# A graph-attention kernel: adding weight tiles by half transfers, finishing a sum one block later, and moving small transfers to another queue

## The chip, the cores and the metric

The kernel runs on one core of one Trainium2 chip. The metric is the device time of one execution in microseconds (us), from the first to the last instruction; lower is better. TensorE (PE) does the matrix products, VectorE (DVE) and ScalarE (ACT) the elementwise work, GpSimd (POOL) issues the transfers that add or cast, SyncE (SP) the plain loads. Each engine works through its own instructions in order and waits on semaphores for the others.

## The reference

Two layers over 4096 nodes with 512 features and 4 heads of 128. The first layer is an encoder and a decoder that share one masked attention; the second is a graph attention network (GAT). Cut to what matters here, the GAT is

```python
feats  = einsum('nf,hfo->hno', X, W)                 # 4 heads of 128
logits = leaky_relu(e_s[:, :, None] + e_n[:, None, :], 0.2)
attn   = softmax(logits + NEG_INF * (1 - A), axis=-1) # 4096 x 4096 for each head
out    = relu(einsum('hnm,hmo->hno', attn, feats) + b)
```

and the encoder's attention, `softmax(sigmoid(f1 + f2))` over the masked neighbours, has the same shape: unnormalised weights for every pair of nodes, a weighted sum of values, and the sum of the weights as the denominator. All of it is float32.

## The kernel before, in words

One function, `attention` (L211), is used three times: as "enc" (the encoder, `kept="write"`), "dec" (the decoder, `kept="read"`, without denominators) and "gat" (the last one, `kept=None`). It walks over 8 blocks, 4 heads times 2 halves of 2048 target nodes. A block has 32 steps `j`, one for each group of 128 source nodes. A step makes one weight tile `e` of 128 sources by 2048 targets (1 MB): in gat ACT does a Relu (L820) and DVE multiplies by the mask tile `a` (L821); in enc ACT does Tanh and Exp (L422, L423) and DVE multiplies (L424). Then PE multiplies the values of the 128 sources with the four 512-wide parts of `e` into four PSUM banks (L352; the fourth bank is taken up at step `EVICT` = 2, and its parts of steps 0 and 1 are done then, L349).

The denominators are the sums of `e` over all sources. A tile can be summed in three ways, and a pair of tuples for each block, `(moved, by_ones)`, says which steps go which way:

- steps in `moved`: a transfer issued by POOL adds the tile onto a second sum tile, `sums2` (L364, with `accum_op` add; the first one only copies). In gat `sums2` is the 1 MB of `w`, named `row0`; in its first block, where `w` still holds the row of scores, it is a tile in device memory, `dacc`, read back into a weight tile at step 30 (L322).
- steps in `by_ones`: PE multiplies the tile by a matrix of ones into the denominators' bank `den` (L304, `add_to_den`).
- all others: DVE adds the tile onto `acc` (L370, L372). In gat `acc` is half of `R[2]`, so these lines read `R<-R,e`.

At the end of the block PE adds `sums2` and `acc` into `den` too. In gat the tuple is `((0, 2, 5, 7, 10, 12, 15, 17, 20, 22, 25), (9, 30, 31))` for every block: 11 tiles by transfer, 3 by ones, 18 by DVE.

Weight tiles rotate through 9 slots (7 and 2 of another pool). A slot is free when PE, DVE and, for a moved tile, the transfer have read it. Mask tiles have 5 slots.

What follows a block is spread over the next block's steps by `at(j, ...)`: eviction of the four banks at step 2 (`out_gat`, ACT, L826), the copy of `den` at `INVERT` = 4 (ACT, L248), and then a chain of small transfers through device memory that turns the sums into a column (`dcol`), inverts it on DVE (L255, L256), stores it (`rinvs`) and spreads it over the partitions (`rb`, four tiles of 256 KB, L262). DVE multiplies by `rb` (L830), ACT adds the bias (L833) and POOL adds the result onto the output in device memory (L839). All these hops are issued by POOL, in the same queue as the moved tiles. The order of instructions within an engine is set when the program is built, from priorities and from `issue_after` pins; it does not change at run time.

Of the kernel before, what the change touches and what calls it, by code (L numbers as in the profile page):

```python
# [31 lines left out]
FP = mybir.dt.float32  # L32
U8 = mybir.dt.uint8
AF = mybir.ActivationFunctionType
ALU = mybir.AluOpType
# [5 lines left out]
IB = 512  # L41
# [4 lines left out]
TB = 2048  # L46
# [15 lines left out]
ENC_FIRST = (), (6, 7, 14, 15, 22, 23, 30, 31)  # L62
ENC_SECOND = (13, 15, 17, 20, 22, 25), (5, 6, 10, 11, 30, 31)
ENC = (0, 2, 5, 7, 10, 12, 15, 17, 20, 22, 25), (8, 9, 30, 31)
GAT = (0, 2, 5, 7, 10, 12, 15, 17, 20, 22, 25), (9, 30, 31)

KEEP = 5

# [13 lines left out]
def kernel(ctx, tc, x, xT, adjT, w0, w0T, v0, wencT, wdecT, vecs, w1, w1T, a1, outT):  # L82
# [65 lines left out]
    ekeep = [[[dram.tile([P, TB], FP, name=f"ekeep{h}_{t}_{k}") for k in range(NJ // KEEP)] for t in range(NTB)]  # L148
             for h in range(H)]

    dacc = dram.tile([P, TB], FP, name="dacc")

    masks = [[dram.tile([MG * P, TB], U8, name=f"mask{t}_{g}") for g in range(NJ // MG)] for t in range(NTB)]

    def everywhere(d, row, lo, n):
# [55 lines left out]
    def attention(what, keep, pools, weights, values, row_of, out, finish, ebufs, modes=None, invert=None,  # L211
# [21 lines left out]
        spool, made, masks0 = pools, 0, list(masks0)  # L233
        if invert is not None:
            acc = spool.tile([P, TB], FP, name="acc") if sums is None else sums
            sums2 = spool.tile([P, TB], FP, name="acc2") if sums2 is None else sums2

        def weight_tile():
            nonlocal made
# [2 lines left out]
                return keep.tile([P, TB], FP, name="e", tag="ek", bufs=EP)  # L242
            return spool.tile([P, TB], FP, name="e", bufs=ebufs)

        def denominators(h, tb, den):

            dsb = spool.tile([P, IB], FP, name="dsb")
            (nc.vector.tensor_copy if kept is not None else nc.scalar.copy)(dsb, den)  # L248
            nc.gpsimd.dma_start(dens[h][tb], dsb[0:P:32, :])
            dcol = spool.tile([P, TB // P], FP, name="dcol", bufs=2)  # L250
            nc.gpsimd.dma_start(dcol, dens[h][tb].rearrange("s (q k) -> (s q) k", k=TB // P))
            return dcol

        def invert_them(h, tb, dcol):
            nc.vector.tensor_scalar(dcol, dcol, invert[0], None, invert[1])  # L255
            nc.vector.reciprocal(dcol, dcol)  # L256
            nc.gpsimd.dma_start(rinvs[h][tb].rearrange("o (p k) -> (o p) k", k=TB // P), dcol)

        def spread(h, tb, s):

            rb = spool.tile([P, IB], FP, name="rb", bufs=2)
            nc.gpsimd.dma_start(rb, everywhere(rinvs[h][tb], 0, s * IB, IB))  # L262
            return rb

        def at(j, f, *args):
# [3 lines left out]
        def ending(h, tb, po, den, slack):  # L269

            outs = [out(spool, h, tb, s, po[s]) for s in range(SB)]
            if den is not None:
                def invert_later():
                    dcol = denominators(h, tb, den)
                    at(INVERT + slack + 6, invert_them, h, tb, dcol)

                at(INVERT, invert_later)
            rbs = {}
            for s, o in enumerate(outs):

                j = INVERT + slack + 7 + s % 2 + s // 2 * 7
                at(j, lambda s=s: rbs.update({s: spread(h, tb, s)}))
                for k, f in enumerate(finish):
                    at(j + 6 + k, lambda f=f, s=s, o=o: f(spool, h, tb, s, o, rbs[s], False))

        def next_row_of(h, tb):
            rowb = keep.tile([P, TB], FP, name="rowb", bufs=2)
# [5 lines left out]
        blocks = [(h, tb) for h in range(H) for tb in range(NTB)]  # L293
        for n, (h, tb) in enumerate(blocks):
            last = n == len(blocks) - 1
            moved, by_ones = modes(n) if modes is not None else ((), ())
            if invert is not None:
                den = bank1()
                begun = False

            def add_to_den(t, stop=False):
                nonlocal begun, last_ones
                for s in range(SB):
                    last_ones = nc.tensor.matmul(den[s * 32:(s + 1) * 32, :], ones[:, 0:32], t[:, s * IB:(s + 1) * IB],  # L304
                                                 start=not begun, stop=stop)
                begun = True

            po, ahead = [bank() for _ in range(SB - 1)], []
            adds, held, back, stores, next_row = [], [], None, [], None
            for j in range(NJ):  # L310

                with pinned(products_of):
                    for f in later.pop(j, []):
                        f()
                with pinned([a_load, *products_of] if j else []):
                    if (n, j) in extras:
                        extras[n, j](a_load)
                    if not last and j == NJ - 10:
                        next_row = next_row_of(*blocks[n + 1])
                if n == 0 and moved and j == NJ - 2:  # L320
                    back = weight_tile()
                    nc.gpsimd.dma_start(back, dacc)  # L322
                e = weight_tile()
                store = j % KEEP == KEEP - 1 and kept is not None
                if store and kept == "read":
                    a_load = nc.sync.dma_start(e, ekeep[h][tb][j // KEEP])
                else:
                    if masks0:
                        a, a_load = masks0.pop(0)
                    else:  # L330
                        a = mask_tile(keep)
                        a_load = load_mask(a, tb, j)
                    products_of = weights(e, rowb, a, j, h, SB if n + j == 0 else 1)
                    if store:
                        stores.append((j // KEEP, e))

                    if j % KEEP == KEEP - 3 and stores:
                        k, t = stores.pop()
                        nc.scalar.dma_start(ekeep[h][tb][k], t)

                def products():
                    nonlocal last_main, last_ones

                    with tc.issue_after(last_ones.ins) if last_ones is not None else nullcontext():

                        if j == EVICT:
                            po.append(bank())
                            for k, t in ahead:
                                nc.tensor.matmul(po[-1], block(values[h], k), t[:, (SB - 1) * IB:SB * IB],  # L349
                                                 start=(k == 0), stop=False)  # L350
                        for s, b in enumerate(po):
                            last_main = nc.tensor.matmul(b, block(values[h], j), e[:, s * IB:(s + 1) * IB],  # L352
                                                         start=(j == 0), stop=(j == NJ - 1))
                    last_ones = None


                early = last and j == NJ - 1 and invert is not None
                if not early:
                    products()
                if j < EVICT:  # L360
                    ahead.append((j, e))
                if invert is not None:
                    if j in moved:
                        nc.gpsimd.dma_start(sums2 if n else dacc, e, **({"accum_op": ALU.add} if j > moved[0] else {}))  # L364
                    elif j in by_ones:
                        held.append(e)
                    else:
                        adds.append(e)
                        if len(adds) == 2:
                            nc.vector.tensor_add(acc, *adds)  # L370
                        elif len(adds) > 2:
                            nc.vector.tensor_add(acc, acc, e)  # L372

                    if held and j + 1 not in by_ones:
                        with tc.issue_after(last_main.ins):
                            for t in held:
                                add_to_den(t)
                        held = []
                    if j == NJ - 1:
                        with tc.issue_after(last_ones.ins) if last_ones is not None else nullcontext():  # L380
                            if moved:
                                add_to_den(sums2 if n else back)
                            add_to_den(acc, True)
                if early:
                    products()
            for k, t in stores:
# [4 lines left out]
            if not last:  # L391

                at(EVICT, ending, h, tb, po, den if invert is not None else None,
                   4 if kept == "write" and n == 0 else 0)
                rowb = next_row
                continue
            outs = [out(spool, h, tb, s, po[s]) for s in range(SB)]
# [4 lines left out]
                        f(spool, h, tb, s, o, rb, True)  # L402
                continue

            inv = spool.tile([P, IB], FP, name="dsb")
            nc.vector.tensor_scalar(inv, den, invert[0], None, invert[1])
            nc.vector.reciprocal(inv, inv)
            if kept is not None:
# [432 lines left out]
    with tc.tile_pool(name="gat", bufs=1) as spool:  # L841
        x1_last = []

        def load_last(load):
# [1 line left out]
            nc.sync.dma_start(x1_last[0], outT[(H - 1) * P:H * P, (NTB - 1) * TB:NTB * TB])  # L846

        attention("gat", spool, spool, gat_weights, v1, lambda h, tb: (rowsg, tb * H + h), out_gat,
                  (scaled_gat, add_to_output), 7, lambda n: GAT, (N * TINY, ALU.add), sums=R[2][:, 0:TB],
                  sums2=row0, row0=row0,  # L850
                  extras={(0, 1): rest_of_rows, (H * NTB - 1, NJ - 10): load_last})


# [40 lines left out]
```

## Time and profile before

| | before |
|---|---|
| time, median of 3 runs | 3289.51 us (3280.21 to 3290.55) |
| profiled run | 3281.28 us, span 3279.5 us, granted clock 0.995 |
| PE busy | 3200.3 us (98%) |
| DVE busy | 2691.2 us (82%) |
| ACT busy | 2598.6 us (79%) |
| gat, block after block | from 2350 us to the end |
| enc, block after block | from 70 us to 1048 us |

Busy time is averaged over stages with different limits, so the table only says that several engines are nearly full. The stages have to be read one by one: the windows of the blocks, the chain of waits, and for each engine what ended its idle time. PE is counted in records, and one 512-wide product in float32 leaves two of them.

### The profile page before, as it was taken

How to read it: one execution, taken by the hardware profiler on the slowest of the kernel's cores; microseconds unless marked ns; L12 is line 12 of the kernel's file. 1: busy time of each engine (PE TensorE's matmuls, PEld its weight loads, DVE VectorE, ACT ScalarE, POOL GpSimd, SP SyncE). 2: the span in 40 equal slices, each digit the busy share in tenths (PEclk: the TensorE clock that was granted, in tenths of full speed). 3: DMA queues.
4: the chain of work that ended last, by engine and by line, in shares of the span. 5: the costliest groups of instructions: out<-in, count | busy, mean ns of one | idle time of the engine just before them, and what ended most of it. 6: DMA issues, size and time to landing. Idle time of an engine off the chain costs nothing.

```text
span 3279.5 us, 25758 instructions
## 1 busy us (share of the span) xinstructions
PE 3200.3 (98%) x8775; PEld 1484.6 (45%) x8775; DVE 2691.2 (82%) x1923; ACT 2598.6 (79%) x1901; POOL 336.7 (10%) x484
## 2 busy tenths in 40 slices
PE   7999999999999999999999999999999999999999
PEld 6334434444443464444444444448644444444443
DVE  6999999999999665655665666586699999999997
ACT  7999999999997449999999999565756666666564
POOL 2000110110110000000000000024201111111111
PEclk9999999999999999999999999999999999999999
DMA  9998988988986013434443444242389789778876
GB/s 208 196 192 226 263 225 231 261 221 231 261 231 171 0 65 126 152 130 136 140 151 131 136 141 138 62 134 72 89 197 225 180 202 226 192 187 207 211 188 155
DMA packets 181028, 564.83 MB, mean 172 GB/s; under 512 B 20452, under 2 KB 23780, under 8 KB 144288
## 3 DMA queue, kind: packets, MB, share of 16 engines
q0 software_dynamic: 43952, 216.38, 34.3%
q1 hardware_dynamic: 126432, 293.72, 26.6%
q10 hardware_dynamic: 10512, 53.08, 4.0%
q8 instruction: 69, 1.13, 0.1%
q14 instruction: 63, 0.52, 0.0%
HBM read 378.15 MB, written 95.82 MB: 145 GB/s over the span
## 4 chain that ended last, share of the span: by engine, by line
PE 64%; DVE 13%; ACT 11%; issue 8%; DMA 4%; POOL 0%; ACTq 0%; DVEq 0%; SPq 0%; POOLq 0%
PE ps L352 50%; PE ps L579 7%; DVE e L424 7%; ACT e L422 6%; ACT e L423 4%; PE ps L763 3%; DVE acc L372 2%; DMA a<-mask 2%; DMA acc<-e 2%; PE den L304 1%; DVE R L372 1%; DVE e L821 1%; PE ps L635 1%; PE ps L349 1%; PE ps L503 1%
## 5 line engine op out<-in xcount | busy, mean ns | idle before, releaser
L352 PE MATMUL ps<-e,R 128*128 128x512 f32 x6048 | 2626.0, 595 | 44.4 <-DVE e L424 36.3
L352 PEld LDWEIGHTS ps<-e,R 128*128 128x128 f32 x6048 | 1145.1, 190 | 1516.7 <-issue 1416.4
L424 DVE TENSOR_TENSOR e<-e,a 128x2048 f32<-128x2048 f32 (+1 forms) x470 | 1052.2, 2260 | 382.0 <-ACT e L423 367.4
L422 ACT ACTIVATE e<-rowb,score 128x2048 f32<-128x2048 f32 (+1 forms) x470 | 912.7, 1968 | 101.8 <-PE ps L352 58.1
L423 ACT ACTIVATE e<-e 128x2048 f32<-128x2048 f32 (+1 forms) x470 | 871.0, 1879 | 6.5
L820 ACT ACTIVATE e<-rowb,nq,jcol 128x2048 f32<-128x2048 f32 x224 | 457.6, 2087 | 231.7 <-DMA w<-e 158.0
L821 DVE SCALAR_TENSOR_TENSOR e<-e,jcol,a 128x2048 f32<-128x2048 f32 (+1 forms) x259 | 591.3, 2317 | 2.6 <-ACT e L820 2.6
L372 DVE TENSOR_TENSOR acc<-acc,e 128x2048 f32<-128x2048 f32 x130 | 297.1, 2286 | 2.1
L372 DVE TENSOR_TENSOR R<-R,e 128x2048 f32<-128x2048 f32 x128 | 292.2, 2283 | 0.0
L579 PE MATMUL ps<-R,w 128*128 128x512 f32 x512 | 220.3, 592 | 0.6 <-DVE w L537 0.6
L262 POOL DMA_DIRECT2D rb<-rinvs x88 | 60.9, 723 | 1076.2 <-DVE R L527 870.5
L579 PEld LDWEIGHTS ps<-R,w 128*128 128x128 f32 x512 | 97.2, 190 | 122.7 <-issue 118.1
L364 POOL DMA_DIRECT2D w<-e x77 | 65.0, 844 | 639.2 <-DMA w<-e 210.4
L364 POOL DMA_DIRECT2D acc<-e x72 | 60.8, 844 | 593.8 <-DMA acc<-e 195.5
L763 PE MATMUL ps<-w1x,hT 128*128 128x260 f32 x512 | 118.5, 391 | 1.8 <-ACT hT L736 1.8
L599 ACT ACTIVATE ex<-ps,bias 128x512 f32<-128x512 f32 x64 | 44.0, 688 | 95.3 <-PE ps L579 78.2
L763 PEld LDWEIGHTS ps<-w1x,hT 128*128 128x128 f32 x512 | 98.6, 194 | 21.6 <-ACT hT L736 3.4
L820 ACT ACTIVATE e<-w,nq,jcol 128x2048 f32<-128x2048 f32 (+1 forms) x35 | 65.3, 1937 | 32.4 <-DMA dacc<-e 32.4
L601 DVE SCALAR_TENSOR_TENSOR ex<-ex,re 128x512 f32<-128x512 f32 x64 | 44.9, 701 | 35.6 <-ACT re L600 35.4
L833 ACT ACTIVATE R<-R,vec 128x512 f32<-128x512 f32 x32 | 23.0, 718 | 60.8 <-DVE R L830 60.6
L768 ACT ACTIVATE R<-ps,rstd 128x128 f32<-128x128 f32 x128 | 38.4, 370 | 38.0 <-PE ps L763 36.9
L304 PE MATMUL den<-e,ones 128*32 128x512 f32 x504 | 61.3, 599 | 0.0
(163 smaller groups left out, 1264.3 us busy)
## 6 DMA issues: line engine op xcount, KB each, us to landing
a<-mask SPq DMA_DIRECT2D x720, 256.0 KB, 3.7
w<-e POOLq DMA_DIRECT2D x77, 1024.0 KB, 8.2
acc<-e POOLq DMA_DIRECT2D x72, 1024.0 KB, 8.8
ekeep<-e ACTq DMA_DIRECT2D x48, 1024.0 KB, 6.2
e<-ekeep SPq DMA_DIRECT2D x48, 1024.0 KB, 4.8
rb<-rinvs POOLq DMA_DIRECT2D x88, 256.0 KB, 5.4
mask<-in_adjT POOLq DMA_DIRECT2D x8, 2048.0 KB, 100.7
rowb<-rows SPq DMA_DIRECT2D x16, 1024.0 KB, 6.5
```

Of the source, the lines that this page charges most:

```text
L262: nc.gpsimd.dma_start(rb, everywhere(rinvs[h][tb], 0, s * IB, IB))
L304: last_ones = nc.tensor.matmul(den[s * 32:(s + 1) * 32, :], ones[:, 0:32], t[:, s * IB:(s + 1) * IB], start=not begun, stop=stop)
L352: last_main = nc.tensor.matmul(b, block(values[h], j), e[:, s * IB:(s + 1) * IB], start=(j == 0), stop=(j == NJ - 1))
L364: nc.gpsimd.dma_start(sums2 if n else dacc, e, **({"accum_op": ALU.add} if j > moved[0] else {}))
L372: nc.vector.tensor_add(acc, acc, e)
L422: nc.scalar.activation(e, rowb, AF.Tanh, bias=column(score[:, 1], j, h), scale=0.5)
L423: last_act = nc.scalar.activation(e, e, AF.Exp, scale=0.5)
L424: last_dve = nc.vector.tensor_mul(e, e, a)
L579: nc.tensor.matmul(z, w[:, fb, o * P:(o + 1) * P], nodes(src[fb], ib), start=(fb == 0), stop=(fb == C - 1))
L763: nc.tensor.matmul(b[:, 0:2 * DX], hT[:, fb, c * P:(c + 1) * P], w1x[:, fb, 2 * k:2 * k + 2, :].rearrange("p h x -> p (h x)"), start=(fb = ...
L820: last_act = nc.scalar.activation(e, rowb, AF.Relu, bias=column(nq, j, h), scale=column(jcol, j, h))
L821: last_dve = nc.vector.scalar_tensor_tensor(e, e, column(jcol2, j, h), a, ALU.add, ALU.mult)
```

## The change

The change has these parts:

1. The transfers that add a moved tile are issued in two halves of 1024 columns each (`in_parts(2, into, e)`). This is in `attention` itself and so holds for enc as well as for gat.
2. In gat the tuples differ by block. The first block moves 13 tiles (even steps 0 to 24) and has two by ones. The middle six blocks move 13 tiles, odd steps 3 to 27, have two by ones, and carry a third entry, `True`. The last block moves 11 tiles, odd steps 3 to 23, and has three by ones as before, 12 in the place of 9.
3. Where the third entry is set, the moved sum is not added to `den` at the end of the block but in step 1 of the next one (`ends_later`).
4. In gat's first block the moved sum is the second half of `R[2]`, on the chip, in the place of `dacc` in device memory; the read back is gone.
5. In gat the hops of the denominators are issued by ACT in the place of POOL (`hop`), and set further apart: store at step 4, column at 7, inversion at 11, store of the inverses at 14, spreading at 15, 16, 20 and 21, scaling three steps after each, output six steps after each. In enc and dec they stay on POOL at the steps they had.
6. `dsb` and `rb` share one tag with 3 slots, where `dsb` had one and `rb` two.

It is for letting each half's transfer run while the other half's completion is awaited, so that more tiles can be summed by transfers, for giving the last of them time to land, and for keeping the small hops out of the queue of the moved tiles.

```diff
-GAT = (0, 2, 5, 7, 10, 12, 15, 17, 20, 22, 25), (9, 30, 31)
+GAT_FIRST = (0, 2, 4, 6, 8, 10, 12, 14, 16, 18, 20, 22, 24), (30, 31)
+GAT = tuple(range(3, 28, 2)), (30, 31), True
+GAT_LAST = (3, 5, 7, 9, 11, 13, 15, 17, 19, 21, 23), (12, 30, 31)
...
-    dacc = dram.tile([P, TB], FP, name="dacc")
...
+        hop = nc.scalar if kept is None else nc.gpsimd
...
-            dsb = spool.tile([P, IB], FP, name="dsb")
+            dsb = spool.tile([P, IB], FP, name="dsb", tag="rb", bufs=3)
             (nc.vector.tensor_copy if kept is not None else nc.scalar.copy)(dsb, den)
-            nc.gpsimd.dma_start(dens[h][tb], dsb[0:P:32, :])
+            hop.dma_start(dens[h][tb], dsb[0:P:32, :])
...
-            rb = spool.tile([P, IB], FP, name="rb", bufs=2)
-            nc.gpsimd.dma_start(rb, everywhere(rinvs[h][tb], 0, s * IB, IB))
+            rb = spool.tile([P, IB], FP, name="rb", bufs=3)
+            hop.dma_start(rb, everywhere(rinvs[h][tb], 0, s * IB, IB))
...
+                at(INVERT, denominators, h, tb, den)
+                at(INVERT + (0 if hop is nc.gpsimd else 3), columns, h, tb, dcols)
+                at(INVERT + slack + (6 if hop is nc.gpsimd else 7), invert_them, dcols)
+                at(INVERT + slack + (6 if hop is nc.gpsimd else 10), inverses, h, tb, dcols)
...
-                j = INVERT + slack + 7 + s % 2 + s // 2 * 7
+                j = INVERT + slack + (7 if hop is nc.gpsimd else 11) + s % 2 + s // 2 * (7 if hop is nc.gpsimd else 5)
...
-                    at(j + 6 + k, lambda f=f, s=s, o=o: f(spool, h, tb, s, o, rbs[s], False))
+                    at(j + (6 + k if hop is nc.gpsimd else 3 + 3 * k),
+                       lambda f=f, s=s, o=o: f(spool, h, tb, s, o, rbs[s], False))
...
-                if n == 0 and moved and j == NJ - 2:
-                    back = weight_tile()
-                    nc.gpsimd.dma_start(back, dacc)
...
-                        nc.gpsimd.dma_start(sums2 if n else dacc, e, **({"accum_op": ALU.add} if j > moved[0] else {}))
+                        for into_half, e_half in in_parts(2, into, e):
+                            nc.gpsimd.dma_start(into_half, e_half, **({"accum_op": ALU.add} if j > moved[0] else {}))
...
-                            if moved:
-                                add_to_den(sums2 if n else back)
-                            add_to_den(acc, True)
+                            if moved and not ends_later:
+                                add_to_den(den, into, not begun)
+                                begun = True
+                            add_to_den(den, acc, not begun, not ends_later)
...
+                if ends_later:
+                    at(1, add_to_den, den, into, False, True)
```

More of the change, by code (lines that the diff above doesn't have):

```diff
@@ L235, in attention @@
             acc = spool.tile([P, TB], FP, name="acc") if sums is None else sums
-            sums2 = spool.tile([P, TB], FP, name="acc2") if sums2 is None else sums2
+            sums2 = (spool.tile([P, TB], FP, name="acc2"), None) if sums2 is None else sums2
         def weight_tile():
@@ L243, in weight_tile, with add_to_den, columns, invert_them @@
             return spool.tile([P, TB], FP, name="e", bufs=ebufs)
+        hop = nc.scalar if kept is None else nc.gpsimd
+        def add_to_den(den, t, start=False, stop=False):
+            nonlocal last_ones
+            for s in range(SB):
+                last_ones = nc.tensor.matmul(den[s * 32:(s + 1) * 32, :], ones[:, 0:32], t[:, s * IB:(s + 1) * IB],
+                                             start=start, stop=stop)
         def denominators(h, tb, den):
-            dsb = spool.tile([P, IB], FP, name="dsb")
+            dsb = spool.tile([P, IB], FP, name="dsb", tag="rb", bufs=3)
             (nc.vector.tensor_copy if kept is not None else nc.scalar.copy)(dsb, den)
-            nc.gpsimd.dma_start(dens[h][tb], dsb[0:P:32, :])
+            hop.dma_start(dens[h][tb], dsb[0:P:32, :])
+        def columns(h, tb, dcols):
             dcol = spool.tile([P, TB // P], FP, name="dcol", bufs=2)
[L251 to L257, printed above, removed]
+            hop.dma_start(dcol, dens[h][tb].rearrange("s (q k) -> (s q) k", k=TB // P))
+            dcols.append(dcol)
+        def invert_them(dcols):
+            nc.vector.tensor_scalar(dcols[0], dcols[0], invert[0], None, invert[1])
+            nc.vector.reciprocal(dcols[0], dcols[0])
+        def inverses(h, tb, dcols):
+            hop.dma_start(rinvs[h][tb].rearrange("o (p k) -> (o p) k", k=TB // P), dcols[0])
         def spread(h, tb, s):
-            rb = spool.tile([P, IB], FP, name="rb", bufs=2)
-            nc.gpsimd.dma_start(rb, everywhere(rinvs[h][tb], 0, s * IB, IB))
+            rb = spool.tile([P, IB], FP, name="rb", bufs=3)
+            hop.dma_start(rb, everywhere(rinvs[h][tb], 0, s * IB, IB))
             return rb
@@ L272, in ending @@
             if den is not None:
[L273 to L277, printed above, removed]
+                dcols = []
+                at(INVERT, denominators, h, tb, den)
+                at(INVERT + (0 if hop is nc.gpsimd else 3), columns, h, tb, dcols)
+                at(INVERT + slack + (6 if hop is nc.gpsimd else 7), invert_them, dcols)
+                at(INVERT + slack + (6 if hop is nc.gpsimd else 10), inverses, h, tb, dcols)
             rbs = {}
             for s, o in enumerate(outs):
-                j = INVERT + slack + 7 + s % 2 + s // 2 * 7
+                j = INVERT + slack + (7 if hop is nc.gpsimd else 11) + s % 2 + s // 2 * (7 if hop is nc.gpsimd else 5)
                 at(j, lambda s=s: rbs.update({s: spread(h, tb, s)}))
                 for k, f in enumerate(finish):
-                    at(j + 6 + k, lambda f=f, s=s, o=o: f(spool, h, tb, s, o, rbs[s], False))
+                    at(j + (6 + k if hop is nc.gpsimd else 3 + 3 * k),
+                       lambda f=f, s=s, o=o: f(spool, h, tb, s, o, rbs[s], False))
         def next_row_of(h, tb):
@@ L295, in attention @@
             last = n == len(blocks) - 1
[L296 to L306, printed above, removed]
+            moved, by_ones, *ends_later = modes(n) if modes is not None else ((), ())
+            den = bank1() if invert is not None else None
+            begun = False
+            into = sums2[0 if n else 1] if moved else None
             po, ahead = [bank() for _ in range(SB - 1)], []
-            adds, held, back, stores, next_row = [], [], None, [], None
+            adds, held, stores, next_row = [], [], [], None
             for j in range(NJ):
@@ L376, in attention @@
                             for t in held:
-                                add_to_den(t)
+                                add_to_den(den, t, not begun)
+                                begun = True
                         held = []
@@ L380, in attention @@
                         with tc.issue_after(last_ones.ins) if last_ones is not None else nullcontext():
-                            if moved:
-                                add_to_den(sums2 if n else back)
-                            add_to_den(acc, True)
+                            if moved and not ends_later:
+                                add_to_den(den, into, not begun)
+                                begun = True
+                            add_to_den(den, acc, not begun, not ends_later)
                 if early:
@@ L403, in attention @@
                 continue
-            inv = spool.tile([P, IB], FP, name="dsb")
+            inv = spool.tile([P, IB], FP, name="dsb", tag="rb", bufs=3)
             nc.vector.tensor_scalar(inv, den, invert[0], None, invert[1])
@@ L848 @@
         attention("gat", spool, spool, gat_weights, v1, lambda h, tb: (rowsg, tb * H + h), out_gat,
-                  (scaled_gat, add_to_output), 7, lambda n: GAT, (N * TINY, ALU.add), sums=R[2][:, 0:TB],
-                  sums2=row0, row0=row0,
+                  (scaled_gat, add_to_output), 7, lambda n: (GAT_FIRST, *[GAT] * (H * NTB - 2), GAT_LAST)[n],
+                  (N * TINY, ALU.add), sums=R[2][:, 0:TB], sums2=(row0, R[2][:, TB:N]), row0=row0,
                   extras={(0, 1): rest_of_rows, (H * NTB - 1, NJ - 10): load_last})
```

## The prediction

> **What bounds the kernel now.** The change touches gat (all parts) and enc (the halves), so I read those two stages: first the windows of the blocks, then the chain of waits, then who waited for whom, then timelines of POOL and ACT. Gat's middle blocks and one of enc, with columns PE, PEld, DVE, ACT, POOL, clock, DMA share, GB/s:
>
> ```profile
> 2579.00:2694.00 115.00, 115.00 (x304) 49.56 (x296) 110.58 (x55) 71.36 (x43) 16.81 (x23) 1.00 0.83 199
> 2809.00:2924.00 115.00, 115.00 (x300) 49.57 (x296) 115.00 (x57) 71.10 (x42) 16.97 (x23) 1.00 0.85 205
> ...
> 450.00:570.00 120.00, 116.67 (x308) 49.42 (x304) 114.62 (x64) 119.87 (x65) 13.21 (x18) 1.00 0.86 237
> ```
>
> In gat PE has no gap and DVE hardly one; ACT has 44 us to spare. In enc ACT is full. Which of gat's two full engines sets the pace, the chain (start, length, what) says:
>
> ```profile
> 2455.14 2.36 DVE e L821
> 2457.50 0.04 issue
> 2457.54 3.70 PE ps L352 x8
> ...
> 2576.07 3.57 PE den L304 x32
> 2579.64 5.35 PE ps L352 x12
> 2584.99 1.72 PE ps L349 x4
> 2586.71 27.47 PE ps L352 x64
> 2614.17 1.00 PE den L304 x8
> 2615.17 75.73 PE ps L352 x176
> 2690.90 3.57 PE den L304 x32
> ```
>
> DVE carries the chain through the first block only, up to 2457.5; from there PE does, every block 2690.90 - 2576.07 = 114.83 us. All of that is matmuls: 110.3 us of products and five sums by ones, one alone (1.00 us, step 9) and four together (3.57 us, 0.89 each: steps 30 and 31, `w`, `acc`). So gat gets faster by what is taken off PE, and by nothing else.
>
> How near are the others? From the starts and ends of each `e`'s instructions in the trace: DVE finishes `e` 0.1 us before PE starts on it at the end of block 0 (there step 31 takes 4.43 us on PE in place of 3.43), 0.5 us at the end of block 2, 5.4 us at the end of block 6. ACT is 8 to 19 us ahead of DVE in blocks 2 and 3, 2.7 us at least in block 6; ACT's lead over PE as a whole stays near 22 us, which is the ring of 9 tiles. What holds ACT and POOL:
>
> ```profile
> POOL w L364 <- DMA w<-e: 210.4, 30, 8.4
> ACT e L820 <- DMA w<-e: 158.0, 46, 6.6
> POOL w L364 <- PE den L304: 134.0, 5, 29.0
> ACT R L833 <- DVE R L830: 60.6, 23, 8.3
> DVE R L830 <- DMA rb<-rinvs: 10.3, 6, 4.4
> ```
>
> The transfers are a loop of their own: each add waits for the one before it to land. Two of them on POOL:
>
> ```profile
> 2601.68 0.86 POOL L364 DMA_DIRECT2D w<-e  x1 [7.29 <-DVE dcol L255]
> 2610.23 0.86 POOL L364 DMA_DIRECT2D w<-e  x1 [7.70 <-issue]
> ```
>
> 8.55 us from one to the next, for 2.5 steps of 3.43 = 8.6 us: just in time, and why they sit 2 or 3 steps apart.
>
> **What the Trainium skill says.** DMA: Bandwidth & Descriptors, section "Anatomy of one DMA", gives a transfer a fixed part of about 2 us, mostly waiting for the receipt, and says that waits are made by the issuing sequencer before dispatch. The trace agrees: the packets of one add (128 of 8 KB, median 629 ns, 8 to an engine: 5.0 us) fill about 5 to 6 of the 8.55 us. The same page, "Rules for kernel authors", calls splitting into two transfers pointless, since both use the same 16 engines; that speaks of bandwidth, and here it is latency that is to be hidden. It also tells that an accumulate must wait for the earlier one on the same bytes, so each half keeps its own chain. "Queues, rings and completion order" has the engines take turns between queues packet by packet, so masks on SP's queue are slowed by adds, not shut out.
>
> **Part by part.** *One sum by ones fewer.* Middle blocks: four sums, three together at the end (2.68) and `w` alone in step 1 (1.00), against 4.57: -0.89 us, six times, -5.3 us. Block 0: four together, the lone one gone: -1.00. The last block has five as before. In block 0 DVE also loses one add of 2.28 us, which ends the wait of 1.0 us at its step 31. Gat: 5.3 + 1.0 + 1.0 = **-7.3 us**, all on the path.
>
> *DVE* loses one add in each of seven blocks (18 to 17 tiles; the first add takes two): 7 x 2.283 = 16 us. PE sets the pace, so beyond that 1.0 us this only widens DVE's lead, by 2.28 - 0.89 = 1.4 us a block.
>
> *More transfers.* 13 tiles at one per two steps, 6.86 us. Whole tiles at 8.55 couldn't; halves overlap one half's receipt with the other's packets, leaving the 5.0 us of packets. Masks take 128 packets of about 100 ns a step, 0.8 us per engine, 1.6 per pair: 6.6 of 6.86 us. The four `rb` (180 ns packets, 1.4 us each), four outputs (0.8 each) and one row (2.8) come on top, some 12 us a block, so up to about 12 us of lag builds up by step 27 and drains in the seven light steps after. DMA share: two more tiles are 10 us of 114, so 0.83 becomes about 0.92. Queued behind POOL's waits are only later halves and outputs. A tile is then held up to 8 + 12 + 5 (the first copy waits for PE's step 1) = 25 us; nine steps give 31, less ACT's 2.1. It fits with some 4 us left. For PE's step 1, tile 27 has six steps, 20.6 us, plus DVE's lead and the sums at the end: 25 or more against 20. No wait expected.
>
> *Hops on ACT.* Seven issues a block; ACT's issue of `ekeep` in enc took 0.33 us, so 2.3 us of 44 spare. Their waits: the store of the inverses at step 14 waits for DVE's step 11, so it bounds ACT's lead to three steps (10 us); step 15 waits for that store to land. Landings of such small ones took 5.1 to 8.4 us from POOL beside adds (the medians of `dcol` and `rinvs`); I take 4, with 2 (the page's fixed part) and 8 as bounds, since ACT's queue has no adds ahead of them. Behind it stands the Relu of step 15, for which DVE waits only if ACT's three steps are used up. L833 may now lag DVE by three steps where it had one, so the 60.6 us shrink. Net nothing on the path. `dacc`'s removal and the shared slots: hidden by the same leads.
>
> *Halves in enc.* ACT is the bound there, so its waits count; first ACT's longest in the timeline of block 1, then all of enc's in the waits:
>
> ```profile
> 307.27 3.90 ACT L422 ACTIVATE e<-rowb,score 128x2048 f32<-128x2048 f32 x2 [2.45 <-DMA acc<-e]
> ```
>
> ```profile
> ACT e L422 <- DMA acc<-e: 5.6, 6, 2.4
> ```
>
> At most 5.6 us to win, at worst nothing or a little lost to 72 more issues on POOL (13 us busy of 120 a block, so not on the path). I take **-3.0**.
>
> The median of 3289.5 lies at the upper end of runs at 3280.2 and 3290.6, so I start from the three runs' mean, 3286.8: 3286.8 - 7.3 - 3.0 = **3276.5 us**.
>
> **Rivals.** *A, gains but within the noise* (0.28): gat gives 6.3 and enc nothing, from the upper level: 3289.5 - 6.3 = 3283. For it: DMA is fuller, and the order of enc's instructions is made anew. *B, the transfers become the bound, slower* (0.12): halves bring no overlap, 8.55 us per tile. The lag at tile 27 is 12 x (8.55 - 6.86) = 20 us, plus 5 and a landing of 8 = 33, against 25 for PE's step 1: PE waits about 6 us in six blocks: 3286.8 - 10 + 36 = 3313. For it: the page's rule and a DMA share near 0.92; against it: only 5.0 us of each 8.55 are packets. *C, ACT's hops or a late mask starve DVE* (0.08): a stall of 8 us in place of 4, with ACT's lead of 2.7 us as in block 6, costs some 2 to 3 us a block beyond DVE's lead: 7 x 2.5 - 7 = +10, 3298. Against it: DVE's lead is largest, over 15 us, just where ACT's is least.
>
> **How the numbers follow.** My case has 0.52. Faster by over 0.3% means under 3279.6: my case less its upper noise, 0.52. Within 0.3% is A, 0.28, and slower B and C, 0.20. For the range: low, all of enc's 5.6 won from the lower level, 3280 - 7.3 - 5.6 = 3267; high, C, 3298; B's tail is left out.
>
> **What would show it.** Right: gat's blocks in the chain at about 113.9 us with sums x24 at the end and x8 after step 0; 264 records of L304 in gat in place of 320; L372 R<-R,e x121; PE's idle still under 2 us; DMA share about 0.92 there; POOL's adds of two halves about 7 us apart. Wrong: gaps of PE or chain pieces of DMA `w<-e` before the sum in step 1 (B), DVE waiting for ACT's L820 or for a mask (C), enc's blocks longer than 120 us.

## The result, and the profile after

The changed kernel takes 3274.64 us (median of six runs, 3273.59 to 3276.20) against 3287.11 us before (median of six, 3279.42 to 3290.55): a ratio of 0.9967, 95% interval 0.9953 to 0.9981, or some 11 us (the medians alone differ by 12.5). 3276.5 was forecast. The six runs of before lie 11 us apart, those of the changed kernel 2.6; whether that is a property of the kernel is taken up with e4. Each ratio below is to runs of the kernel before that belong to the same experiment; their medians are 3284.9 to 3287.1 us.

In the lines of the changed kernel L359 is the product that was L352, L356 the late one for the fourth bank (L349), L252 the sum by ones (L304), L833 ACT's Relu (L820), L834 DVE's product (L821), L839 the eviction (L826), L373 the adding transfer (L364), L843 and L846 the scaling and the bias (L830, L833); in enc L435 and L437 stand for L422 and L424.

The windows of two of gat's middle blocks and one of enc, with the columns as in the prediction (PE, PEld, DVE, ACT, POOL, clock, DMA share, GB/s):

```profile
2578.00:2692.00 114.00, 114.00 (x289) 49.31 (x289) 114.00 (x57) 76.06 (x46) 25.53 (x30) 1.00 0.95 225
2806.00:2920.00 114.00, 114.00 (x293) 49.34 (x296) 110.41 (x55) 72.05 (x41) 25.54 (x30) 1.00 0.93 221
450.00:570.00 120.00, 117.18 (x313) 49.58 (x305) 115.08 (x64) 119.87 (x66) 22.80 (x31) 1.00 0.88 237
```

PE is as full as it was, in windows that are one us shorter; POOL's issues and the share of the DMA engines have grown (in gat from 0.83 and 0.85 to 0.95 and 0.93). The chain of waits (start, length, what) over the end of block 1 and all of block 2:

```profile
2572.61 2.71 PE den L252 x24
2575.33 2.77 PE ps L359 x6
2578.10 1.00 PE den L252 x8
2579.09 2.77 PE ps L359 x6
2581.87 1.72 PE ps L356 x4
2583.58 103.00 PE ps L359 x240
2686.58 2.71 PE den L252 x24
```

A block is 2686.58 - 2572.61 = 113.97 us, against 114.83. Three sums stand at its end, the moved one alone after the next block's step 0, and the lone sum that stood at step 9 is gone: products run through in one piece of 103.00 us. From block 0 on the chain holds PE alone. The waits in gat (us in total, times, longest):

```profile
POOL w L373 <- DMA w<-e: 383.3, 136, 6.9
ACT e L833 <- DMA w<-e: 136.6, 44, 5.8
ACT R L846 <- DVE R L843: 16.8, 18, 2.8
DVE e L834 <- ACT e L833: 10.8, 7, 2.6
```

POOL waits more often and shorter (136 times, as each half has its chain), ACT's waits for the scaling fell from 60.6 to 16.8 us, and DVE now has to wait for ACT at times. None of that reaches PE: from gat's first product to its last group of sums it has no gap.

For all experiments, two stretches were taken from PE's records in each profile: enc from its first product to the start of its last group of sums, and gat likewise.

| kernel | enc, us | gat, us | ACT's waits in enc for `acc<-e`, us |
|---|---|---|---|
| before | 976.1 | 915.1 | 5.6 |
| before, second profile (e0) | 983.3 | 915.9 | 13.0 |
| changed | 975.1 | 909.2 | 5.4 |
| e1 halves only | 975.5 | 915.1 | 5.6 |
| e2 whole tiles in gat | 978.7 | 935.8 | 8.4 |
| e3 hops on POOL | 976.5 | 908.3 | 6.2 |
| e4 whole tiles in enc | 985.0 | 909.1 | 14.1 |

### The profile page after: what moved, and what is told of

The parts are those of the page before. It is cut to its first block, busy times and chain, and to the rows that moved or that the text cites. A ratio compares the mean times of both kernels' runs of the same rounds, so it can differ in the third digit from the quotient of the medians.

```text
span 3271.8 us, 26021 instructions
## 1 busy us (share of the span) xinstructions
PE 3196.2 (98%) x8719; PEld 1484.0 (45%) x8719; DVE 2675.9 (82%) x1916; ACT 2600.1 (79%) x1901; POOL 465.7 (14%) x622
## 4 chain that ended last, share of the span: by engine, by line
PE 73%; DVE 10%; ACT 7%; issue 5%; DMA 5%; POOL 0%; DVEq 0%; ACTq 0%; SPq 0%; POOLq 0%
PE ps L359 58%; PE ps L592 7%; DVE e L437 6%; ACT e L435 4%; PE ps L776 3%; DMA a<-mask 3%; ACT e L436 2%; DVE acc L381 2%; DMA acc<-e 2%; PE den L252 1%; PE ps L356 1%; PE ps L648 1%; PE ps L516 1%; DMA rinvs<-dcol 1%; PE ps L498 0%
## 5 line engine op out<-in xcount | busy, mean ns | idle before, releaser
L359 PE MATMUL ps<-e,R 128*128 128x512 f32 x6048 | 2628.8, 595 | 40.3 <-DVE e L437 32.9
L359 PEld LDWEIGHTS ps<-e,R 128*128 128x128 f32 x6048 | 1147.0, 191 | 1512.8 <-issue 1420.0
L437 DVE TENSOR_TENSOR e<-e,a 128x2048 f32<-128x2048 f32 (+1 forms) x470 | 1052.4, 2261 | 381.3 <-ACT e L436 367.1
L435 ACT ACTIVATE e<-rowb,score 128x2048 f32<-128x2048 f32 (+1 forms) x470 | 912.7, 1968 | 102.1 <-PE ps L359 58.1
L833 ACT ACTIVATE e<-rowb,nq,jcol 128x2048 f32<-128x2048 f32 x224 | 460.8, 2089 | 269.2 <-DMA w<-e 136.6
L834 DVE SCALAR_TENSOR_TENSOR e<-e,jcol,a 128x2048 f32<-128x2048 f32 (+1 forms) x259 | 593.0, 2332 | 10.8 <-ACT e L833 10.8
L381 DVE TENSOR_TENSOR R<-R,e 128x2048 f32<-128x2048 f32 x121 | 278.0, 2298 | 0.0
L373 POOL DMA_DIRECT2D w<-e x178 | 150.3, 847 | 609.4 <-DMA w<-e 383.3
L373 POOL DMA_DIRECT2D acc<-e x144 | 120.4, 880 | 540.8 <-DMA acc<-e 222.9
L277 POOL DMA_DIRECT2D rb<-rinvs x60 | 34.2, 574 | 1062.5 <-DVE R L540 871.6
L833 ACT ACTIVATE e<-w,nq,jcol 128x2048 f32<-128x2048 f32 (+1 forms) x35 | 65.7, 1938 | 30.8 <-DMA R<-e 30.8
L787 POOL TENSOR_TENSOR vacc<-vacc,R 128x128 f32<-128x128 f32 x120 | 53.0, 468 | 57.5 <-ACT R L781 57.5
L252 PE MATMUL den<-e,ones 128*32 128x512 f32 x440 | 53.0, 598 | 0.0
```

Of the source, the lines that this page charges most:

```text
L373: nc.gpsimd.dma_start(into_half, e_half, **({"accum_op": ALU.add} if j > moved[0] else {}))
L435: nc.scalar.activation(e, rowb, AF.Tanh, bias=column(score[:, 1], j, h), scale=0.5)
L437: last_dve = nc.vector.tensor_mul(e, e, a)
L787: nc.gpsimd.tensor_add(vacc[:, h, :], vacc[:, h, :], block(v1[h], j))
L833: last_act = nc.scalar.activation(e, rowb, AF.Relu, bias=column(nq, j, h), scale=column(jcol, j, h))
L834: last_dve = nc.vector.scalar_tensor_tensor(e, e, column(jcol2, j, h), a, ALU.add, ALU.mult)
```

## The experiments

**The kernel before once more, and halves alone.** My theory was that gat pays for PE's work and nothing else; the rival, that the halves themselves are the gain. e0 is the kernel before without an edit.

> The kernel before, once more, for a second profile of it: its six runs lie between 3279.4 and 3290.6 us while the six of the changed kernel lie within 2.6 us. If gat is bound by PE alone, its blocks 1 to 6 take 114.8 us in this profile too, and what differs between a short and a long run lies elsewhere; if DVE's lead, which falls to 0.1 us at the end of block 0, sometimes runs out, gat's blocks are longer in a long run.

It took 3287.73 us in the median (3283.39 to 3290.36), and its profile is of a run at the upper end, span 3288.6. Gat's stretch is the same within 0.8 us, and 7.2 us are in enc. The 0.8 us are blocks 2 and 3, with 115.44 and 115.03 us in place of 114.83: here DVE holds the chain up to 2696 us, two blocks longer than in the first profile, and finishes the last tile of both blocks only 0.1 us ahead of PE. So DVE's lead can run out in gat, at a small price. Timeline of ACT in enc, in the first profile and then in e0, and of POOL in e0:

```profile
378.08 2.00 ACT L422 ACTIVATE e<-rowb,score 128x2048 f32<-128x2048 f32 x1 [0.39 <-DMA acc<-e]
...
389.31 3.88 ACT L422 ACTIVATE e<-rowb,score 128x2048 f32<-128x2048 f32 x2
```

```profile
381.68 2.00 ACT L422 ACTIVATE e<-rowb,score 128x2048 f32<-128x2048 f32 x1 [4.20 <-DMA acc<-e]
...
396.63 3.90 ACT L422 ACTIVATE e<-rowb,score 128x2048 f32<-128x2048 f32 x2 [3.62 <-DMA acc<-e]
```

```profile
382.12 0.88 POOL L364 DMA_DIRECT2D acc<-e  x1 [10.35 <-DVE e L424]
397.10 0.85 POOL L364 DMA_DIRECT2D acc<-e  x1 [14.10 <-DMA acc<-e]
```

One add of a whole tile holds the next up for 15.0 us, where the median landing is 8.8; ACT, the bound of this stage, stands still twice behind such slots, for 4.20 and 3.62 us. In the first profile it waited 0.39 us at the first of the two places and not at all at the second. That is the main difference between these two profiles; that it makes the whole spread of the kernel before isn't shown.

```diff
-                        nc.gpsimd.dma_start(sums2 if n else dacc, e, ...)
+                        for into_half, e_half in in_parts(2, sums2 if n else dacc, e):
+                            nc.gpsimd.dma_start(into_half, e_half, ...)
```

> Before with the moved tiles in halves, in enc and gat, nothing else changed. Theory (PE sets gat's pace, one sum by ones fewer is the gain): gat's blocks stay at 114.8 us, enc wins 0 to 3 us, so 3284 to 3287 beside a before of 3287. Rival (the halves themselves are the gain): most of the 12 us, 3275 to 3278.

3280.83 us (3279.14 to 3284.46), ratio 0.9985 (0.9979 to 0.9992). Gat's blocks stayed at 114.83 us, so the rival falls; but the time is 4 to 5 us lower than that of before (4.1 by the medians, 4.9 by the ratio), somewhat more than the 0 to 3 us that I gave enc. That this gain lies in enc follows from gat's unchanged blocks; the one profile of e1, with 975.5 us, doesn't show it against the first of before.

**Whole tiles, in gat or in enc.** Each undoes the halves in one stage of the changed kernel.

```diff
-                        for into_half, e_half in in_parts(2, into, e):
+                        for into_half, e_half in in_parts(1 if kept is None else 2, into, e):   # e2
+                        for into_half, e_half in in_parts(2 if kept is None else 1, into, e):   # e4
```

> The changed kernel with whole tiles in gat (halves stay in enc): 13 tiles at one per two steps without overlap. Theory: each tile takes about 8.5 us for 6.86, the lag grows to some 20 us, and PE waits for the moved sum in step 1 of the next block, about 6 us in six blocks: 3300 to 3313. Rival (the transfers have room anyway, halves bring nothing in gat): 3273 to 3277.

3300.62 us (3297.64 to 3306.40), ratio 1.0051 (1.0036 to 1.0066): slower than both kernels, at the lower edge of what the theory gave. But the wait isn't the one that I had named. Timeline of PE at a block's boundary:

```profile
2708.16 1.07 PE L252 MATMUL den<-w,ones 128*32 128x512 f32 x8 [1.84 <-DMA w<-e]
2709.15 2.84 PE L359 MATMUL ps<-e,R 128*128 128x512 f32 x6
2714.88 2.92 PE L356 MATMUL ps<-e,R 128*128 128x512 f32 x4 [2.89 <-ACT R L839]
```

```profile
2700.18 4.08 ACT L833 ACTIVATE e<-rowb,nq,jcol 128x2048 f32<-128x2048 f32 x2 [6.00 <-DMA w<-e]
2708.20 6.06 ACT L833 ACTIVATE e<-rowb,nq,jcol 128x2048 f32<-128x2048 f32 x3 [3.93 <-DMA w<-e]
2714.17 2.39 ACT L839 ACTIVATE R<-ps,ssum 128x512 f32<-128x512 f32 x4
```

PE waits 1.84 us for the moved sum, and then longer for a PSUM bank that ACT has not evicted. ACT's evictions stand in its queue behind Relus that wait for weight slots, and those are held by the late transfers. PE's own waits for the two, over all of gat:

```profile
PE ps L356 <- ACT R L839: 15.6, 5, 5.9
PE den L252 <- DMA w<-e: 2.5, 2, 1.8
```

So PE stood still 15.6 us for evictions at step 2 and 2.5 us for `w` in step 1. The lag that I had worked out is there; it reaches PE mostly through ACT's queue. And the pauses cost twice: at four of them the granted clock is 0.5 for 3.4 or 6.8 us, 17 us in all. If half of that is lost, an estimate, 15.6 + 2.5 + 8.5 = 26.6 us account for gat's stretch, 935.8 us in place of 909.2.

> The changed kernel with whole tiles in enc (halves stay in gat). Theory: the halves in enc are worth some 4 us and the spread, since a single late transfer stalls ACT there, so 3277 to 3281 with a spread of 6 us or more. Rival (enc's difference is chance of two profiles): 3274 to 3276, spread 3 us.

3282.78 us (3276.91 to 3286.01), ratio 0.9987 (0.9980 to 0.9994): 0.20% above the changed kernel, and 1.8 us above what the theory gave. Enc's stretch, 985.0 us, is the longest of all, with ACT's waits of 4.20 and 3.52 us at the same two places as in e0. So the halves in enc are worth some 4 to 7 us, and not by chance of two profiles: 4 to 5 by e1, and by e4 against the changed kernel 6.6 from the two ratios (8.1 from the medians). These two kernels ran in different experiments, and the intervals of their ratios touch (0.9980 and 0.9981).

They shorten the waits and don't end them: in the profiles of eleven kernels with halves in enc ACT's waits come to 3.7 to 8.7 us, in the three with whole tiles to 5.6, 13.0 and 14.1. Nine of the eleven still have 1.6 to 4.7 us at the first of the two places, none more than 1.0 us at the second.

The spread isn't settled by this. Its 20 runs lie 9.1 us apart, but with a standard deviation of 1.9 us, against 1.6 in e1 (20 runs), 2.5 in e9 (10 runs, halves in enc) and 3.1 in the 39 runs of before that go with e4. So whole tiles in enc alone don't bring back the spread of before, and other kernels with halves in enc spread more widely than the six runs of the changed kernel (standard deviation 1.1).

**What a sum by ones costs, and how far that goes.** All edits are in the tuples.

```diff
-GAT = tuple(range(3, 28, 2)), (30, 31), True
+GAT = tuple(range(3, 28, 2)), (29, 30, 31), True    # e5
+GAT = tuple(range(3, 28, 2)), (31,), True           # e6
+GAT = tuple(range(3, 30, 2)), (31,), True           # e7
+GAT = tuple(range(3, 28, 2)), (30, 31)              # e8
```

> The changed kernel with step 29 by ones too in the six middle blocks (29, 30, 31), so DVE has an add less. Theory: PE sets the pace and a sum in a group costs it 0.89 us: 6 x 0.89 = 5.3 us longer, 3280, blocks of 114.85 us. Rival (DVE sets the pace): 13 us shorter or no longer.

3281.33 us (3279.12 to 3285.23), ratio 0.9986 (0.9979 to 0.9993). Blocks of 114.83 us, with four sums at the end where the changed kernel has three: 0.86 us each. DVE had one add of 2.3 us less in each block and nothing came of it, so DVE doesn't set the pace.

> The changed kernel with step 31 alone by ones in the six middle blocks, step 30 added by DVE. PE loses 0.89 us a block, DVE gains 2.28 us. If PE still sets the pace: 3269.3, blocks of 113.1 us. If DVE becomes the bound once its lead is used up: between 3270 and 3277, and the chain goes over DVE.

3270.97 us (3269.70 to 3274.72), ratio 0.9954 (0.9939 to 0.9969). Blocks of 113.11 us: 0.86 less, and PE still carries the chain:

```profile
2575.13 1.85 PE den L252 x16
...
2688.24 1.85 PE den L252 x16
```

DVE has no idle time left in the windows, and yet its lead over PE at the blocks' ends grows by 0.7 us a block, from 3.6 to 7.1.

> The changed kernel with 14 tiles moved (3 to 29) and step 31 alone by ones in the middle blocks; DVE as in the changed kernel. If the transfers still keep up: 3269.3. If not: their lag grows by some 5 us a block's end, ACT's Relus wait for slots, and evictions queued behind them hold PE at step 2, as with whole tiles: 3275 or more.

3270.18 us (3270.12 to 3274.17), ratio 0.9953 (0.9938 to 0.9968), so no different from e6. Four of the six middle blocks take 113.1 us, block 2 116.6. DMA share is 0.98 to 0.99, and at the boundary ahead of block 2 the timeline of PE has both waits of e2 in small:

```profile
2575.28 1.05 PE L252 MATMUL den<-w,ones 128*32 128x512 f32 x4
2577.61 1.05 PE L252 MATMUL den<-w,ones 128*32 128x512 f32 x4 [1.28 <-DMA w<-e]
2578.60 2.84 PE L359 MATMUL ps<-e,R 128*128 128x512 f32 x6
2582.39 1.98 PE L356 MATMUL ps<-e,R 128*128 128x512 f32 x4 [0.95 <-ACT R L839]
```

PE did the matmuls of the first half of `w` (four records) and stood still for the second half. At 14 tiles the transfers are near their limit.

> The changed kernel with the moved sum taken up at the end of the block again, not in the next block's step 1. Theory: the last add is issued some 15 us before the end of the block and lands in time, and four sums together cost 3.57 for 2.71 + 1.00, so 3272.5 to 3275. Rival (the later sum is what gives the last tile time to land): PE waits at each block's end, 3280 or more.

3273.97 us (3269.30 to 3275.38), ratio 0.9960 (0.9945 to 0.9975): by the medians the same as the changed kernel, but the chain shows a small difference in each block:

```profile
2573.91 3.57 PE den L252 x32
2577.47 5.35 PE ps L359 x12
2582.82 1.72 PE ps L356 x4
2584.54 103.00 PE ps L359 x240
2687.54 3.57 PE den L252 x32
```

113.63 us, no wait for the last tile. With 13 tiles in halves, taking the sum up a block later gains nothing and costs 0.34 us: a sum alone is 1.00 us and cuts the products in two, in a group it is 0.86.

**The hops.** e3 leaves them on POOL at the steps of before; e9 has them on ACT at those steps.

```diff
-        hop = nc.scalar if kept is None else nc.gpsimd
+        hop = nc.gpsimd                                                     # e3
...
-                at(INVERT + (0 if hop is nc.gpsimd else 3), columns, h, tb, dcols)
+                at(INVERT + 0, columns, h, tb, dcols)                       # e9, and so at the other steps
```

> The changed kernel with gat's hops left on POOL's queue, at the steps they had before. Theory: the hops lie beside PE's work on either queue, so 3273 to 3278, though ACT's waits for L830 grow. Rival (freeing POOL's queue is what makes room for 13 tiles): the waits of the hops hold up the halves, lag runs into step 1, 3282 or more.

3276.20 us (3271.58 to 3278.32), ratio 0.9972 (0.9959 to 0.9984); gat's stretch 908.3 us against 909.2. Block 0 is 1.4 us shorter in this profile for another reason (a shorter spell of half clock, taken up under block 0 below), so the other blocks took 0.5 us longer than with the hops on ACT, in blocks 2 and 3. The rival falls: POOL has room for the hops and 13 tiles in halves.

> The changed kernel with the hops on ACT's queue but at the steps they had on POOL, close together. Theory: ACT stands still for each landing (about 5 us three times a block) with the Relus behind it; its lead over DVE of 2 to 10 us is used up in some blocks, and 3276 to 3290 follow. Rival (hidden wherever they stand): 3274 to 3276.

3276.40 us (3271.63 to 3278.61), ratio 0.9969 (0.9960 to 0.9979), gat 908.3 us, where all of the difference to 909.2 is in block 0. Here my theory fell. ACT's lead over DVE is used up at moments (DVE waited 12.3 us for it in all, eight times), but DVE was 3 to 13 us ahead of PE in those blocks, and PE didn't notice. Neither the hops' queue nor their distance brings or costs anything that these runs can tell.

**A version that beats both.** Taking the two findings together:

```diff
-GAT = tuple(range(3, 28, 2)), (30, 31), True
-GAT_LAST = (3, 5, 7, 9, 11, 13, 15, 17, 19, 21, 23), (12, 30, 31)
+GAT = tuple(range(3, 28, 2)), (31,)                                         # e10
+GAT = tuple(range(3, 30, 2)), (), True                                      # e11
+GAT_LAST = (3, 5, 7, 9, 11, 13, 15, 17, 19, 21, 23), (30, 31)               # both
```

> What the runs point to: middle blocks with 13 moved and step 31 alone by ones, all three sums at the end of the block (2.71 us in place of 2.71 and 1.00); last block with 30 and 31 by ones, 12 added by DVE. If PE still sets the pace, blocks of 112.8 us, 1.2 us less than the changed kernel's six times, and 1.0 less in the last: 8 us, 3266.5. If DVE's 18 tiles a block (113 us at most) take over: 3269 to 3271.

3268.89 us (3264.36 to 3270.19), ratio 0.9943 (0.9929 to 0.9956); gat 900.0 us, 9.2 less than in the changed kernel's profile, of which 1.4 are again the shorter spell of half clock. The chain has four of the blocks at 112.78 us, as worked out:

```profile
2801.26 2.71 PE den L252 x24
2803.98 5.35 PE ps L359 x12
2809.32 1.72 PE ps L356 x4
2811.04 103.00 PE ps L359 x240
2914.04 2.71 PE den L252 x24
```

Block 2 took 113.4 us, with Relus of ACT and an eviction behind them in the chain at its start. The enc stretch of this profile was 977.4 us, ordinary; the median is 2.4 us above my figure, within its runs' spread.

> One further: 14 moved, none by ones in the middle blocks, DVE 18 tiles, the moved sum in the next block's step 1; last block as in e10. PE alone would come to 112.2 us a block, 3263. But the transfers have 14 tiles (one of seven blocks already stood still for 3.5 us with 14), DVE is full and the sum of acc waits for the add of step 31: 3265 to 3275, with waits of PE for w or for ACT's evictions.

3268.04 us (3265.62 to 3270.33), ratio 0.9941 (0.9923 to 0.9958), gat 900.6 us, with the longer spell. No sum by ones is left in the middle blocks, yet by the runs it is no faster than e10: the blocks behind the second take 112.3 to 113.1 us, and the second 114.3, with DVE's adds and the transfers in its chain. In these profiles PE, DVE and the transfers all stand near their limits.

## Why the prediction was right

**PE sets gat's pace, a sum by ones fewer is the gain: right, and its size too.** 0.89 us a block was predicted for the six middle blocks, 0.86 was measured (114.83 to 113.97), 5.2 us for 5.3. e5, e6, e8 and e10 move it by the predicted steps in both directions, and e1, which leaves the sums alone, leaves gat at 915.1 us.

**Block 0: mis-sized in the profile shown.** 2.0 us were predicted, 0.8 measured (114.77 to 114.01 from PE's first product to its sums). The DVE wait at the end did go, as predicted. What came in its place is at the other end: PE stands idle for 5 us ahead of gat in both kernels, and its granted clock drops to half. Timeline of PE there, before and then in the changed kernel:

```profile
2346.41 4.30 PE L352 MATMUL ps<-e,R 128*128 128x512 f32 x6 [4.98 <-DVE e L821]
```

```profile
2344.90 5.46 PE L359 MATMUL ps<-e,R 128*128 128x512 f32 x6 [4.99 <-DVE e L834]
```

The first six records take 5.46 us in the changed kernel's profile, and 4.30 before with the same work. The clock's records give 0.5 for 10.2 us in the first (2340.8 to 2351.0) and for 6.8 us in the second (2342.6 to 2349.4). In e3, e6, e7, e8 and e10, with 6.8 us at half clock, block 0 takes 112.6 us, 2.2 less than before, so the step holds; the changed kernel's profile had the longer spell (more on it at the end).

**Halves in enc: the right mechanism, the term too small.** I put 3.0 us, with 5.6 as the most, since that was all that ACT waited for these transfers. That ceiling came from one profile, of a run at 3281 us; in one at 3290 us ACT waited 13.0. By e1 and e4 the term is 4 to 7 us. The start was good: the mean of the three runs, 3286.8, lies within 0.4 us of the later median of six, where their own median was 2.4 too high. A gat term 1.4 us too large for that profile and an enc term 1 to 4 us too small then cancelled in part, so it is partly luck that the total came out within 2 us.

**The transfers: right that 13 tiles need halves and that halves fit.** The share rose to 0.93 to 0.95 (0.92 forecast). First halves are issued 7.5 us apart on average in block 4, and ACT's least lead over PE from block 1 on, from the end of a Relu to PE's first product on its tile, is 15.6 us, against 16.2 before (13.6 in e0): there was more room than the 4 us that I had left. The Trainium skill's page DMA: Bandwidth & Descriptors, section "Rules for kernel authors", advises against two transfers to disjoint halves of the partitions, since both run on the same 16 engines. The halves here are halves of the columns, and no run here tries halves of the partitions; splitting by columns is worth 26 us of gat (e2), because each add waits for the one before and a second chain fills that time.

**Rival B: right that slow transfers would cost much, wrong on the way and high in the size.** It priced PE's waits at 36 us (6 a block, where its own 33 against 25 would give 8) and had them in step 1, for the moved sum. e2 shows 26 us, most of it at step 2, through evictions queued behind ACT's waiting Relus. **Rival C** didn't occur, not even with the hops close together (e9). The argument that the prediction put against it held: DVE's lead over PE is a second buffer behind ACT's lead over DVE. It was the theory of e9 that left that buffer out. **The hops and the later sum**: no gain, as e3, e9 and e8 show. The new place of block 0's sum and the shared slots weren't tried by themselves.

## What to carry to other kernels

Where one engine carries the chain without a gap, price a change by what it takes off that engine alone, at the price of the place it has there: a small product in a group cost 0.86 us, alone 1.00. Here a chain of accumulating transfers was paced by its landings (8.55 us from one to the next, 5.0 us of it packets), and two chains of halves raised its rate; where such a chain falls behind, look for the stall in what is queued behind the waits of the engine that refills the buffers. And when runs of a kernel spread, take a second profile before taking one profile's waits as the most there is to win.

## What the hardware showed unexpectedly

An add of 1 MB in enc kept the next one waiting some 15 us where 8.8 is the median landing, at the same step in two different kernels (e0, e4) and not in the first profile of before. The starts of the DMA packets show where the time went. In e0 two other transfers of 1 MB were issued beside the add: ACT's store of `ekeep` 0.4 us ahead of it and SP's load of `rowb` 0.07 us after it. The store's packets started from 383.0 to 386.9 us, the load's from 386.5 to 391.8, and the add's from 389.7 to 395.5, the first of them 7.6 us after the add's issue (7.5 us in e4, with the same order). In the first profile of before the load was issued 3.9 us after the add, and the order was store (379.0 to 381.4), add (381.6 to 387.8), load (388.3 to 391.5); that add landed after 10.6 us. So transfers of 1 MB went through nearly one after the other, and the late add stood behind two. This is read from three profiles; no run moved the load.

After PE's pause ahead of gat its granted clock stayed at 0.5 for 6.8 us in ten profiles and for 10.2 us in four (the changed kernel, e4, e5, e11), and nothing between, though most of these kernels have the same instructions up to there (the changed kernel, e5 and e11 as well as e3 and e6 to e10): 1.4 us of block 0 hang on which of the two it is. The clock's records show what goes with it. In each profile all spells of half clock start on one grid of 3.413 us and last one to four of its steps, but for the one at the very end; 6.8 and 10.2 us are two and three steps. In the ten profiles the spell begins 1.0 us or more after PE fell idle (1.0 to 1.2, and 2.4 in e9), in the four 0.7 to 0.9 us after. So it goes by where the pause falls on the grid, which differs from profile to profile.
